# Second block of an attention kernel walked downwards, and its weight loads issued from ScalarE

## The chip, the cores and the metric

One core of a Trainium2 chip runs the whole program. The metric is the device time of one execution in microseconds; the kernel before was run three times, and the median counts.

## The reference, cut to what matters

The input is 16 sequences of 256 tokens with 256 features, in float32. One transformer layer is computed:

```
h   = layernorm(x)
q, k, v = h @ W_Q + b_Q, h @ W_K + b_K, h @ W_V + b_V     # 16 heads of 128
att = softmax(causal(q k^T / sqrt(128)))
y   = concat_heads(att v) @ W_O + b_O
x   = x + layernorm(y)
h   = layernorm(x)                                        # 256 -> 2048 -> 256
f   = (gelu(h @ Wg^T) * (h @ Wu^T)) @ Wd^T                # weights unpacked from 4-bit codes
x   = x + layernorm(f)
```

## The kernel before

**Precision.** Most products are made of float32 operands that are split into a high and a low part, so that one product is three matmuls (`mm3`: high*high, high*low, low*high). Splitting is an engine's work (a copy for the high part, a subtraction for the low part), so split weights are written to DRAM once and later loaded ready-made.

**Blocks, pairs, units.** The 4096 tokens are cut into `NBLK` = 8 blocks of `TB` = 512. Within a block the 16 heads are taken in `NG` = 8 pairs, and a pair gives two units, one for each head: 128 units in all. A numbered pair `p` is block `p // 8`, place `p % 8`; `head_pair(p)` says which two heads stand there. The main loop runs over `i`, one unit for each turn, as a software pipeline: in turn `i` the program records K and Q of unit `i+5` (`st_qk`), scores and softmax of unit `i+4` (`st_s`), V for unit `i+4` (`st_v`, or `st_v1` and `st_v2`), the transposition of the probabilities (`st_t`), the way of the transposed probabilities out to DRAM (`st_w`, four writes `hop<-tr`) and back (`st_b`, one load `pt<-hop`), their split (`st_p`), the product with V (`st_z`, whose result goes to `pz` and then through ScalarE to `zh`), and the product with W_O (`st_o`). After the attention come 32 groups of the feed-forward part, which use no K, Q or O weights and reuse V's and O's buffers.

**V.** V is computed for two head pairs at a time, over four units, under a key `w`. Keys of the first block (`w < 4`) use the plain form `st_v`: six matmuls of 512 columns in each of four units. Later keys use a form with seven products instead of eight (`st_v1`, `st_v2`): 42 matmuls of 256 columns over the four units, with sums in `vv` made by ScalarE and VectorE, and with the split left to `v_split` (ScalarE copies `vh`, GpSimd subtracts `vl`). Weights for the seven products are seven tiles wide (`WD[.., "v"]`, 896 KB for each part), for the plain form four.

**Weights.** Each of K and Q together (`WKQ`, 1024 KB), O (`WO`, 512 KB) and V (`WV`, two parts of 896 KB) has two buffers in SBUF. In block 0 the weights are made there and kept in DRAM (`w_keep`, `v_keep`, `v_keep_sums`). From block 1 on `w_get` loads them. The call `weights((p + 4, "kq"))` stands at the end of each even turn, `weights((p + 1, "o"), (p + 5, "v"))` at the end of each odd one. `DOWN` names the blocks that take the pairs in falling order: where a block falls and the one before it rises (or the reverse), the first two pairs and the first two V keys are those that still lie in the buffers, and `w_get` loads nothing for them (`back`). Before, `DOWN` is 2, 4, 6: block 1 rises like block 0 and begins with fresh loads.

**Order.** Every compute instruction goes through `run`, which holds it behind the instruction recorded last on each engine; every DMA goes through `dma`, which issues from SyncE (SP) and holds it behind the DMA issued last. So an engine's order, and SP's, is the order of the program. A DMA also takes one of eight semaphores in turn, and an issue waits until the DMA that last had the same semaphore has landed. Small jobs (layer norms, unpacking of feed-forward weights, sums) are fed in at `slot` calls.

Of the kernel before, what the change touches and what calls it, by code (L numbers as in the profile page):

```python
# [15 lines left out]
ALU = mybir.AluOpType  # L16
# [5 lines left out]
NBLK = NT // TB  # L22
NG = 8
# [5 lines left out]
def kernel(  # L29
# [19 lines left out]
    nc = tc.nc  # L49
# [11 lines left out]
    def f(ap):  # L61
        return ap.bitcast(F32)
# [24 lines left out]
    def dma(dst, src):  # L87
        if queue[0] is None:
            queue[0] = nc.sync.dma_start(dst, src).ins
            return  # L90
        with tc.issue_after(queue[0]):
            queue[0] = nc.sync.dma_start(dst, src).ins
# [3 lines left out]
    def run(op, dst, *args, **kw):  # L96
        with ExitStack() as behind:
            for m in last.values():
                behind.enter_context(tc.issue_after(m))
            ins = op(dst, *args, **kw)  # L100
        last[ins.ins.engine] = ins.ins
        return ins
# [23 lines left out]
    def add(jobs, job, kind):  # L126
        jobs.append([job, 0, kind])

    def overdue(time):
        while late and late[0][0] <= time:  # L130
            _, do, args = late.popleft()
            do(*args)
# [165 lines left out]
    W = {}  # L298
    RAW = {}
    WD = {}  # L300
# [2 lines left out]
    WO = wp.tile([P, 2, 2, 512], F32R, tag="wo", name="wo", bufs=1)  # L303
    WV = wp.tile([P, 2, 3584], F32R, tag="wv", name="wv", bufs=1)

    DOWN = range(2, NBLK, 2)

    def slot_of(p):
        return (p % NG + max(p // NG - 1, 0)) % 2

    def v_slot(w):
        return (w % (NG // 2) + max(w // (NG // 2) - 1, 0)) % 2

    def head_pair(p):
        b, at = divmod(p, NG)
        return NG - 1 - at if b in DOWN else at

    RAWV = {}

# [13 lines left out]
    def w_view(w):  # L333
        return w.rearrange("p s (k c) -> p s k c", k=2)
# [74 lines left out]
    def split(p, n):  # L409
        w_split(p, n)  # L410
        yield from ()

    def w_get(p, n):

        if p < NG:
            add(splits, split(p, n), A_ if n in "vo" else V_)
        elif p < len(pairs):
            overdue(now[0] + 4)
            g, back = head_pair(p), p % NG < 2 and p >= 2 * NG
            if n == "v":  # L420
                key, part = p // 2, p % 2
                at = key % (NG // 2)
                if at < 2 and p >= 2 * NG:
                    W[key, n] = W[key - 1 - 2 * at, n]
                    return
                W[key, n] = w = WV[:, v_slot(key)].rearrange("p (s m c) -> p s m c", s=2, m=7)
                dma(f(w[:, part]), WD[g // 2, n][:, part])
                return
            before = p - 1 - 2 * (p % NG)
            if n == "kq":  # L430
                w = WKQ[:, slot_of(p)]
                if not back:
                    dma(f(w), WD[g, n])
                for m in range(2):
                    W[p, n[m]] = W[before, n[m]] if back else w_view(w[:, m])
            else:
                w = WO[:, slot_of(p)]
                if not back:
                    dma(f(w), WD[g, n])
                W[p, n] = W[before, n] if back else w_view(w)  # L440

    MOVING_LAST = ((0, 0), (1, 0), (0, 1))
    STATIONARY_LAST = ((0, 0), (0, 1), (1, 0))
# [1 line left out]
    def mm3(o, terms, passes=STATIONARY_LAST, start=True, stop=True, shared=False, lows_last=False):  # L445

        todo = [(lhs(a), rhs(c)) for lhs, rhs in terms for a, c in passes]
        if lows_last:
            todo = [todo[m] for m in (0, 1, 3, 4, 2, 5)]
        for i, (lhs, rhs) in enumerate(todo):  # L450
            run(
                nc.tensor.matmul, o, lhs, rhs, start=start and i == 0, stop=stop and i == len(todo) - 1, skip_group_check=shared
            )


    units = [(b, NG - 1 - g if b in DOWN else g, j) for b in range(NBLK) for g in range(NG) for j in range(2)]
    N = len(units)
    pairs = [(b, g) for b in range(NBLK) for g in range(NG)]
    Q, K, V, PR, TR, HOP, PT, PH, Z, PO = {}, {}, {}, {}, {}, {}, {}, {}, {}, {}

    after = deque()
# [71 lines left out]
    def v_split(w, g, bi):  # L533
        c = slice(g * 256, (g + 1) * 256)
        vh, vl = (t[:, bi, c] for t in V[w][0:2])
        run(nc.scalar.copy, vh, vv[:, v_first(g, bi)])
        run(nc.gpsimd.tensor_tensor, vl, vv[:, v_first(g, bi)], f(vh), ALU.subtract)
# [26 lines left out]
    def st_v3(k):  # L564

        w, r = divmod(k, 4)
        w, g, bi = ((w - 1, 1, 0), (w, 0, 0), (w, 1, 1), (w, 0, 1))[r]
        if NG // 2 <= w < N // 4:
            v_split(w, g, bi)

    def st_v(k):
# [87 lines left out]
    def st_z(u):  # L659
        b, g, j = units[u]  # L660
        ph, pl, pt = PH.pop(u)
        vh, vl, vr = V[u // 4]
        at = 2 * (g % 2) + j
        e = slice(at * E, (at + 1) * E)
        pz = ps.tile([P, TB], F32, tag="pz", name="pz")
        for bi in range(2):
            o = pz[:, bi * S : (bi + 1) * S]
            mm3(o, [(lambda a: (vh, vl)[a][:, bi, e], lambda c: (ph, pl)[c][:, :, bi, :])], MOVING_LAST, stop=False)
            run(nc.tensor.matmul, o[:, P:], vr[:, bi, e], pt[:, 4 + bi], start=False, stop=True)
        zh = work.tile([P, TB], F32R, tag="zh", name="zh", bufs=3)  # L670
        zl = work.tile([P, TB], F32R, tag="zl", name="zl", bufs=3)
        bias = bqk[:, 2, 2 * g + j : 2 * g + j + 1]
        run(nc.scalar.activation, zh, pz, AF.Identity, bias=bias)
        after.append((nc.vector.scalar_tensor_tensor, zl, pz, bias, f(zh), ALU.add, ALU.subtract))
        Z[u] = (zh, zl)

    def st_o(p, dh):
# [151 lines left out]
    def f_tile(n):  # L829
        w = wp.tile([P, 2, 8, P], F32R, tag="fs", name="wu", bufs=2)  # L830
        if n == "d":
            return w.rearrange("p s m c -> p (s m c)")[:, 0:1024].rearrange("p (s k c) -> p s k c", s=2, k=2)
        return w

    FGD = {}

    def f_place(k, n):

        if n == "u":
            return f_tile(n)  # L840
        at = k + (n == "d")
        if at not in FGD:
            FGD[at] = WV[:, at % 2]
        if n == "g":
            return FGD[at][:, 0:2048].rearrange("p (s m c) -> p s m c", s=2, m=8)
        return FGD[at][:, 2048:3072].rearrange("p (s k c) -> p s k c", s=2, k=2)
# [351 lines left out]
    for i in range(-5, N + 2):  # L1198
        p = i // 2
        odd = i % 2 == 1  # L1200
        if p >= 0 and not odd and p < len(pairs):
            b, g = pairs[p]
            if g == 0 and b + 1 < NBLK:
                add(urgent, ln1(b + 1), N_)
            if b == 0 and g == 6:
                pieces = [(fg, n) for fg in range(NG) for n in "gud"]
                f_load(*pieces[0])
            if b == 0 and g == 7:
                for m, piece in enumerate(pieces):
                    add(idle, f_make(*piece, pieces[m + 1] if m + 1 < len(pieces) else None), V_)  # L1210
            if b == NBLK - 1 and g == 0:
                add(spare, x_ops(0), N_)
        if 0 <= i + 4 < N:
            st_s(i + 4)
        while after:
            run(*after.popleft())
        if 2 * NG <= i + 4 < N:
            st_v1(i + 4)
        slot(V_)
        if i + 5 < N:  # L1220
            st_qk(i + 5)
        else:
            finished.append(i)
        st_v3(i + 4)
        slot(V_, urgent, behind)
        slot(G_)
        slot(G_ + A_)
        if 0 <= i + 4 < N:
            st_t(i + 4)
        if i == N:  # L1230
            await_(X[0], "last", spare)
            X[0].pop("last")()
        if i >= N - 4:
            part(0, ("m1", "m2", "m6", "m5", "m7", "m3")[i - (N - 4)])
        if 0 <= p - 1 < len(pairs):
            st_o(p - 1, i % 2)
        if 0 <= i + 1 < N:
            st_p(i + 1)
        if 0 <= i + 4 < 2 * NG:
            st_v(i + 4)  # L1240
        elif 0 <= i + 4 < N:
            st_v2(i + 4)
        if 0 <= i < N:
            st_z(i)
        if 0 <= i + 3 < N:
            st_b(i + 3)
        if 0 <= i + 4 < N:
            st_w(i + 4)
        if odd:
            weights((p + 1, "o"), (p + 5, "v"))  # L1250
        else:
            weights((p + 4, "kq"))
        slot(A_ + G_)
        if N - 9 <= i < N - 7:
            f_get(0, "ug"[i - (N - 9)])
# [7 lines left out]
    for k in range(NGRP):  # L1263
        sb, g = divmod(k, NG)
# [88 lines left out]
```

## Time and profile before

| what | value |
|---|---|
| median of three runs | 1516.76 us (1514.41 to 1520.52) |
| the profiled execution, its own time | 1516.03 us |
| its span, first to last instruction | 1514.2 us |
| TensorE matmul (PE) busy | 1489.1 us, 98% |
| VectorE (DVE) / ScalarE (ACT) / GpSimd (POOL) busy | 1158.3 / 1111.2 / 728.3 us |
| moved by DMA | 391.89 MB, 76.7% of the time of 16 DMA engines on queue q1 |
| mean granted TensorE clock | 0.997 |
| loads and stores of `wkq` / `wo` | 52 / 52 issues from SP |
| seven-product loads of `wv` | 32 issues from SP |

Busy time of PE counts pipelined matmuls, so 98% says that PE seldom waits, not that it works at its peak. The profile is read here by the distance in time between equal points of two units: where nothing waits, that distance repeats exactly, and what a stretch has above it was lost. "SPq" is SP issuing a DMA.

### The profile page before, as it was taken

The numbers are of one execution on the slowest core, as the hardware profiler recorded it, in microseconds if no ns is written. First come the engines' busy times: TensorE is split into PE (matmuls) and PEld (weight loads), VectorE is DVE, ScalarE is ACT, GpSimd is POOL, SyncE is SP. The second block draws the span as 40 slices with busy tenths as digits, with TensorE's granted clock in tenths as the row PEclk, the third lists the DMA queues.
The fourth block names the chain that finished last, engine by engine and source line by source line (L and its number), as shares of the span: only waits on it lengthen the run. The fifth ranks groups of instructions, "written<-read, shape, count | busy, mean of one in ns | idle before, by whom it ended". The sixth has DMA issues, their size and how long they took to land.

```text
span 1514.2 us, 26690 instructions
## 1 busy us (share of the span) xinstructions
PE 1489.1 (98%) x8335; PEld 1297.3 (86%) x8335; DVE 1158.3 (76%) x3020; ACT 1111.2 (73%) x2804; POOL 728.3 (48%) x1041
## 2 busy tenths in 40 slices
PE   8999999999999999999999999999999999999997
PEld 7888888998899998899999889987888888888886
DVE  6775787777787787778778777767887787787876
ACT  6987777887887787787888777775666665666665
POOL 5876667767768867866786876630000000000000
PEclk9999999999999999999999999999999999999999
DMA  7999997898799699699789879875647465655561
GB/s 261 350 329 306 323 332 246 271 294 288 230 306 322 215 308 311 220 304 301 248 266 315 283 229 302 285 265 208 236 167 275 172 248 197 247 182 203 218 235 52
DMA packets 186991, 391.89 MB, mean 259 GB/s; under 512 B 19808, under 2 KB 127840, under 8 KB 169952
## 3 DMA queue, kind: packets, MB, share of 16 engines
q1 hardware_dynamic: 186848, 390.17, 76.7%
q8 instruction: 66, 1.08, 0.3%
q14 instruction: 77, 0.63, 0.1%
HBM read 275.28 MB, written 114.82 MB: 258 GB/s over the span
## 4 chain that ended last, share of the span: by engine, by line
PE 78%; DMA 9%; DVE 4%; POOL 3%; ACT 3%; issue 1%; SPq 1%; DVEq 0%; ACTq 0%; POOLq 0%
PE pd L100 13%; PE pk L100 9%; PE po L100 9%; PE pq L100 9%; PE pa L100 8%; PE pv L100 8%; PE pz L100 8%; PE sc L100 7%; PE pf L100 5%; PE pe L100 2%; DMA wv<-wv 2%; DVE sum L100 1%; DMA ohop<-oback 1%; POOL pr L100 1%; DMA o<-ohop 1%
## 5 line engine op out<-in xcount | busy, mean ns | idle before, releaser
L100 POOL TENSOR_SCALAR pr<-pr,rc 128x128 f32<-128x128 f32 (+1 forms) x512 | 219.6, 446 | 128.0 <-DVE rc L100 123.9
L100 DVE CUSTOM_DVE_ANT_0 sc<-sc,mask 128x128 f32<-128x128 f32 (+1 forms) x512 | 180.7, 374 | 114.9 <-PE sc L100 106.2
L100 POOL TENSOR_TENSOR rs<-rs,mhalf 128x4 f32<-128x4 f32 (+1 forms) x35 | 33.8, 965 | 480.6 <-DVE rs L100 271.8
L100 ACT ACTIVATE pr<-sc,mn 128x128 f32<-128x128 f32 (+1 forms) x512 | 207.8, 418 | 68.9 <-DVE mn L100 68.8
L100 PE MATMUL pv<-wv,xT 128*128 128x256 f32 (+1 forms) x1272 | 196.7, 291 | 3.1 <-DVE vv L100 2.9
L100 PE MATMUL pk<-xT,wkq 128*128 128x512 f32 x768 | 199.0, 394 | 0.4 <-DMA wkq<-wkq 0.4
L100 PE MATMUL pq<-xT,wkq 128*128 128x512 f32 x768 | 196.0, 391 | 0.0
L100 PEld LDWEIGHTS pv<-wv,xT 128*128 128x128 f32 x1272 | 177.8, 190 | 14.5 <-DVE vv L100 4.0
L100 PEld LDWEIGHTS pq<-xT,wkq 128*128 128x128 f32 x768 | 145.1, 189 | 30.9
L100 POOL TENSOR_TENSOR pl<-pt,ph 128x512 fp32r<-128x512 f32 x124 | 159.7, 1288 | 21.9 <-ACT ph L100 21.8
L100 ACT COPY part<-pa 128x512 f32<-128x512 f32 x192 | 111.6, 585 | 67.7 <-PE pa L100 65.0
L100 ACT ACTIVATE zh<-pz,bqk 128x512 fp32r<-128x512 f32 x128 | 88.4, 690 | 95.3 <-PE pz L100 95.0
L100 PE MATMUL po<-zh,wo 128*128 128x512 f32 x512 | 157.7, 389 | 0.0
L100 PEld LDWEIGHTS pk<-xT,wkq 128*128 128x128 f32 x768 | 136.3, 190 | 23.1 <-DMA wkq<-wkq 0.6
L100 DVE SCALAR_TENSOR_TENSOR kl<-pk,bqk,kh 128x512 fp32r<-128x512 f32 x128 | 95.7, 748 | 57.6 <-ACT kr L100 56.1
L100 POOL TENSOR_TENSOR vl<-vv,vh 128x256 fp32r<-128x256 f32 x112 | 83.4, 744 | 107.1 <-ACT vh L100 106.1
L100 DVE STREAM_TRANSPOSE tr<-pr 128x768 f32<-128x768 f32 x128 | 123.5, 965 | 6.6 <-DMA hop<-tr 5.4
L100 PEld LDWEIGHTS po<-zh,wo 128*128 128x128 f32 x512 | 96.1, 188 | 20.0
L100 PE MATMUL sc<-kr,qr 128*128 128x128 f32 x512 | 99.5, 275 | 6.1 <-ACT qr L100 6.1
L100 ACT ACTIVATION_READ_ACCUMULATOR pr<-sc,mn 128x1 f32 x512 | 103.9, 203 | 0.0
L100 DVE TENSOR_TENSOR sum<-sum 128x512 f32<-128x512 f32 x128 | 87.9, 686 | 17.9 <-ACT sum L100 17.6
L100 PE MATMUL po<-zl,wo 128*128 128x512 f32 x256 | 99.9, 390 | 0.9 <-DVE zl L100 0.9
(158 smaller groups left out, 3990.0 us busy)
## 6 DMA issues: line engine op xcount, KB each, us to landing
wkq<-wkq SPq DMA_DIRECT2D x52, 1024.0 KB, 6.4
hop<-tr SPq DMA_DIRECT2D x512, 96.0 KB, 3.7
pt<-hop SPq DMA_DIRECT2D x128, 384.0 KB, 5.2
wu<-fu SPq DMA_DIRECT2D x32, 1024.0 KB, 8.6
wv<-fg SPq DMA_DIRECT2D x32, 1024.0 KB, 5.7
wv<-wv SPq DMA_DIRECT2D x32, 896.0 KB, 6.5
wo<-wo SPq DMA_DIRECT2D x52, 512.0 KB, 4.7
wv<-fd SPq DMA_DIRECT2D x32, 512.0 KB, 3.5
```

Source lines behind the costliest of these rows:

```text
L100: ins = op(dst, *args, **kw)
```

## The change

1. `DOWN` becomes 1, 3, 5, 7. The order within a falling block keeps the two pairs of one V key in rising order (6, 7, 4, 5, 2, 3, 0, 1). Each block from 1 on now begins with the two pairs and the two V keys that lie in the buffers, so `back` holds for block 1 too; slots become `p % 2`.
2. The V keys 4 and 5 (the first half of block 1) are those of block 0 that still lie there in the plain form, so the plain form is used for six keys (`PLAIN = 6`) instead of four.
3. `w_get` issues its loads from ScalarE (`run(nc.scalar.dma_start, ...)`), in ScalarE's own order, instead of from SP. Loads drop from 44 + 44 + 32 (K/Q, O, V parts) to 42 + 42 + 28.
4. In the last five units the low part `zl` is recorded at once instead of at the start of the next turn.
5. The feed-forward buffers in `WV` swap places.

```diff
-    DOWN = range(2, NBLK, 2)
+    DOWN = range(1, NBLK, 2)
+    PLAIN = 6
     def slot_of(p):
-        return (p % NG + max(p // NG - 1, 0)) % 2
+        return p % 2
     def v_slot(w):
-        return (w % (NG // 2) + max(w // (NG // 2) - 1, 0)) % 2
+        return (w % (NG // 2) + w // (NG // 2)) % 2
     def head_pair(p):
-        return NG - 1 - at if b in DOWN else at
+        return NG - 2 - at // 2 * 2 + at % 2 if b in DOWN else at
...
     def w_get(p, n):
-            g, back = head_pair(p), p % NG < 2 and p >= 2 * NG
+            g, back = head_pair(p), p % NG < 2
...
-                if at < 2 and p >= 2 * NG:
+                if at < 2:
...
-                dma(f(w[:, part]), WD[g // 2, n][:, part])
+                run(nc.scalar.dma_start, f(w[:, part]), WD[g // 2, n][:, part])
...
-                    dma(f(w), WD[g, n])
+                    run(nc.scalar.dma_start, f(w), WD[g, n])
...
     def st_v3(k):
-        if NG // 2 <= w < N // 4:
+        if PLAIN <= w < N // 4:
...
     def st_z(u):
-        after.append((nc.vector.scalar_tensor_tensor, zl, pz, bias, f(zh), ALU.add, ALU.subtract))
+        low = nc.vector.scalar_tensor_tensor, zl, pz, bias, f(zh), ALU.add, ALU.subtract
+        if u + 5 < N:
+            after.append(low)
+        else:
+            run(*low)
...
-            FGD[at] = WV[:, at % 2]
+            FGD[at] = WV[:, (at + 1) % 2]
...
-        if 2 * NG <= i + 4 < N:
+        if 4 * PLAIN <= i + 4 < N:
             st_v1(i + 4)
...
-        if 0 <= i + 4 < 2 * NG:
+        if 0 <= i + 4 < 4 * PLAIN:
             st_v(i + 4)
```

More of the change, by code (lines that the diff above doesn't have):

```diff
@@ L426, in w_get @@
                 W[key, n] = w = WV[:, v_slot(key)].rearrange("p (s m c) -> p s m c", s=2, m=7)
-                dma(f(w[:, part]), WD[g // 2, n][:, part])
+                run(nc.scalar.dma_start, f(w[:, part]), WD[g // 2, n][:, part])
                 return
-            before = p - 1 - 2 * (p % NG)
             if n == "kq":
@@ L432, in w_get @@
                 if not back:
-                    dma(f(w), WD[g, n])
+                    run(nc.scalar.dma_start, f(w), WD[g, n])
                 for m in range(2):
-                    W[p, n[m]] = W[before, n[m]] if back else w_view(w[:, m])
+                    W[p, n[m]] = W[p - 2, n[m]] if back else w_view(w[:, m])
             else:
@@ L438, in w_get @@
                 if not back:
-                    dma(f(w), WD[g, n])
-                W[p, n] = W[before, n] if back else w_view(w)
+                    run(nc.scalar.dma_start, f(w), WD[g, n])
+                W[p, n] = W[p - 2, n] if back else w_view(w)
     MOVING_LAST = ((0, 0), (1, 0), (0, 1))
@@ L453, in mm3 @@
             )
-    units = [(b, NG - 1 - g if b in DOWN else g, j) for b in range(NBLK) for g in range(NG) for j in range(2)]
+    pairs = [(b, g) for b in range(NBLK) for g in range(NG)]
+    units = [(b, head_pair(p), j) for p, (b, _) in enumerate(pairs) for j in range(2)]
     N = len(units)
-    pairs = [(b, g) for b in range(NBLK) for g in range(NG)]
     Q, K, V, PR, TR, HOP, PT, PH, Z, PO = {}, {}, {}, {}, {}, {}, {}, {}, {}, {}
```

## The prediction

> **What bounds the kernel now.** I read the page first, for who is busy.
>
> ```profile
> span 1514.2 us, 26690 instructions
> ...
> PE 1489.1 (98%) x8335; PEld 1297.3 (86%) x8335; DVE 1158.3 (76%) x3020; ACT 1111.2 (73%) x2804; POOL 728.3 (48%) x1041
> ...
> DMA  7999997898799699699789879875647465655561
> ```
>
> PE is the bound: 98% busy, so only what makes PE wait, or gives it other matmuls, moves the end. The DMA row is near full in the first third of the span and falls later. Then I looked for where PE loses time. In the timeline I took the first weight load of each `pk` (one for each unit). Where nothing waits, four units of the seven-product form last 442.53 to 473.27 = 30.74 us, three of them 7.87. The view of windows, cut at such points (columns: length, then busy time of PE, PEld, DVE, ACT, POOL, then granted clock, DMA share, GB/s):
>
> ```profile
> 71.13:102.20 31.07, 31.07 (x179) 27.34 (x178) 22.98 (x66) 27.49 (x75) 22.91 (x30) 1.00 0.97 322
> 102.20:135.48 33.28, 32.41 (x185) 28.23 (x183) 19.91 (x63) 23.73 (x67) 22.16 (x31) 1.00 0.97 319
> 135.48:228.93 93.45, 92.77 (x584) 83.53 (x583) 69.36 (x210) 72.19 (x204) 64.39 (x93) 1.00 0.97 324
> 228.93:248.43 19.50, 17.64 (x103) 15.49 (x102) 12.21 (x41) 13.18 (x37) 14.66 (x21) 0.91 0.93 317
> 248.43:356.33 107.90, 107.77 (x679) 97.28 (x678) 85.35 (x259) 85.87 (x243) 73.97 (x109) 1.00 0.84 266
> 356.33:851.13 494.80, 493.55 (x3107) 446.03 (x3105) 389.35 (x1183) 395.22 (x1107) 362.40 (x524) 1.00 0.87 280
> ```
>
> Row 1 is four plain units with PE never idle: 31.07. Row 2 is four more plain units: 2.2 us lost. Row 3 is twelve units, 3 x 30.74 = 92.22: 1.2 lost. Row 4 is two units, 2 x 7.87 = 15.74: 3.8 lost, at a granted clock of 0.91. So the stretch that ends with the first units of block 2 loses 7.2 us, with DMA at 0.93 to 0.97. After it, row 5 loses 0.6 against 14 units (123.0 - 15.7 = 107.3), row 6 loses 2.8 against 16 x 30.74 = 492.0, and 851.13 to 976.26 loses 2.1: 5.5 us in six blocks.
>
> Next I asked what ends the waits. At the entrance of block 1 the timeline of SP and ACT shows fresh loads in the way:
>
> ```profile
> 109.74 0.45 SPq L92 DMA_DIRECT2D wv<-wv  x1
> ...
> 120.49 0.34 SPq L92 DMA_DIRECT2D wkq<-wkq  x1
> ...
> 121.15 0.63 ACT L100 ACTIVATE wo<-rawo 128x512 fp32r<-128x512 f32 x1 [3.58 <-DMA rawo<-in_wo]
> ```
>
> The chain goes through just these two: the `wv` load took 10.73 us, SP waited for it before `wkq` (120.49), and PE's `pk` waited for that at 126.96. Behind the same `wv`, `rawo` was late, and ACT sat 3.58 us in front of its softmax. At the end of block 1 the chain reads:
>
> ```profile
> 222.61 7.97 DMA o<-ohop
> ...
> 230.60 5.84 DMA hop<-tr
> ...
> 236.62 0.98 DVE tr L100
> ...
> 238.22 0.98 PE pv L100 x6
> ```
>
> A `hop` write waits its turn, the transpose waits for its buffer, DVE's `vv` is late and PE stands still for 1.86 us (timeline). From 239.76 on, for 3.4 us, the granted clock is 0.5, which makes up most of the rest of row 4's 3.8.
>
> **The change part by part.** *Block 1 falls.* Removed: two `wkq`, two `wo` and four `wv` loads, 2 x 1024 + 2 x 512 + 4 x 896 = 6656 KB = 6.8 MB, the last of them issued at 187.40 us. At row 2's 319 GB/s that is 21 us of transfer out of the 126 us from 102.20 to 228.93. Row 2's loss hangs on two of these loads: gone, -2.2. For row 3 the waits are of DVE's `vv` at 186 and 190 us, where SP is 5 to 7 us behind its place in the program: `wkq` is issued at 179.80, its turn's `zh` ended at 173.2. With less queued, -1.2. Row 4's loss has the `o` load, two `xs` loads and an `fu` store in front of the `hop` write, and none of these is removed; but SP came there late (`wo` issued at 220.41, its turn's `zh` ended at 213.0), and in later blocks the same place costs far less: row 6 holds four such places and loses 2.8 in all. I take the whole 3.8 as gone, because a wait that ends before 1.86 us takes the clock's part with it; the bounds are 0 and 3.8.
>
> The granted clock fell after a PE gap of 1.86 us. The page "TensorE: Matmul & The Clock Gate" of the Trainium skill (Part 1: The HAM clock gate) gives an idle window of about 3.4 us as what drops the clock to half. By that rule this gap would have cost only its 1.9 us, and the sum below would be 1.9 us smaller in gain; the trace, with 0.91 in row 4, decides.
>
> *Two keys become plain.* Row 1 against the steady four units: 31.07 - 30.74 = 0.33 for each key, on the path since PE has no gap there: +0.7 for two. What this takes from the others (for a key four `vl` at 0.74 us from POOL, about 1 us net from ACT and 1.3 us net from DVE) is beside PE and counted at nothing; it only adds slack.
>
> *Loads leave SP.* 112 issues. SP's take 0.34 to 0.45 us, median 0.44: 49 us that SP no longer spends in 900. SP mostly waits, for example for `hop` landings (171.6 us in its waits), so its issue time is not the bound in the steady blocks. At the six block ends SP holds the loads back behind a wait for `oback` and `ohop` (up to 10 us after the turn's `zh`); the loads are freed from that, but PE waited for a load there only once (0.13 us at 355.75). The other way round, `hop` and `pt` are freed from the loads in front of them. I take 1 of the 5.5 us of the later blocks as gained; the bounds are 0 and 3, since 2.1 us of PE's waits are for POOL's `vl`, which is not SP's.
>
> The page "DMA: Bandwidth & Descriptors" (section "Issuing engines are not separate DMA queues") speaks against this part: transfers issued by two engines share the 16 DMA engines, and only issue time is saved. By that rule this part is 0 and the gain 1 us smaller.
>
> *ACT issues.* No DMA is issued by ACT in the trace, so the price is bounded: nothing, or SP's 0.44 us each, 49 us of ACT. The place is after `zh`, ahead of the next unit's four `pr` exponentials, `kh`, `kr`, `qh`, `qr` and `ph`, which all queue behind it. There ACT is idle in most turns:
>
> ```profile
> 664.85 0.69 ACT L100 ACTIVATE zh<-pz,bqk 128x512 fp32r<-128x512 f32 x1 [0.81 <-PE pz L100]
> 666.41 0.37 ACT L100 ACTIVATE pr<-sc,mn 128x128 f32<-128x128 f32 x1 [0.87 <-DVE mn L100]
> ```
>
> One issue (even turns) or two (odd) take 0.44 or 0.88 of that 0.87. Behind it `qr` ends at 163.05 and PE wants it at 164.47 (timeline of block 1): 1.4 us more. So up to 0.87 + 1.4 = 2.3 us in a turn cost nothing; I take 0, being nearest to the 0.88. No wait on PE comes with it: the buffers' last readers run ahead of `pz` in PE's order, which `zh` has waited for. What comes is the wait for the eighth DMA before it. In the changed program's order that is in most cases a `hop` write of the turn before, landed long before (median 3.7 us), and never one that stands behind the `ohop` of the same turn.
>
> The loads now start up to 2 us earlier, beside the `hop` writes (660.10 against a `zh` end of 658.4). At 323 GB/s a `wkq` is 3.2 us; a `hop` delayed by that still lands within the two turns (15.7 us) that two `tr` buffers give. Cost 0; it becomes real where DVE's `tr` waits, four times and 5.4 us in all before.
>
> *`zl` at once, `WV` swapped.* VectorE's order in the two built programs is the same at the end, since nothing was recorded between the two places: the 0.9 us wait of PE for `zl` at 1006 stays. 0 for both.
>
> Sum: -2.2 - 1.2 - 3.8 + 0.7 - 1.0 = -7.5. The profiled execution took 1516.03 (span 1514.2 and 1.8 around it), 0.7 under the median of the runs. 1516.03 - 7.5 = **1508.5 us**.
>
> **The rivals.** *Half of it stays.* Row 4 is made by `o`, `xs` and `fu` ahead of `hop`, which the change leaves in SP's queue, and the second queue brings nothing. Then -2.2 - 1.2 + 0.7 = -2.7, or -1.5 if row 3 stays as well: 1513 to 1514.5, no change that counts. For it: the chain names those three, no weight load. Against: the steady blocks have the same three and lose little.
>
> *More comes back.* The loads' own queue also empties SP at every block end: 3 of the 5.5 us there, and the sum is -9.5: 1506.5 or somewhat less.
>
> *ACT becomes the waiter (slower).* One mechanism: an issue on ACT waits for a landing that SP itself has delayed, and everything behind `zh` waits with it. SP is 7 to 10 us late at each of six block ends (`wo` at 349.5, its turn's `zh` ended at 340.1). If ACT inherits half of that, 4 us, less the 2.3 us of cover, it costs 1.7 us in each of three turns at each of six ends, 31 us; less the gain of 7.5: 1539.5, and with two of the three turns 1529. It decides from 2.3 us of wait in a turn on. For it: ACT is 73% busy and keeps strict order; a PE gap of 2 us also costs clock. Against: the program's order of the eighth DMA before, as above.
>
> **How the numbers follow.** The forecast has 0.46; its own range is 1505.5 to 1511.5. Half stays: 0.20. More comes back: 0.15. ACT waits: 0.19. About 0.5% is what a measurement of this kernel can tell from no change, 7.6 us from the median, which is 1509.2 and 1524.3. The forecast lies across the first: 0.30 of its 0.46 faster, 0.16 the same. Half stays is all the same, more comes back all faster, ACT waits 0.17 slower and 0.02 the same. So faster has 0.30 + 0.15 = 0.45, the same 0.16 + 0.20 + 0.02 = 0.38, slower 0.17. The range 1503 to 1521 takes in the first three cases with the bounds of their terms and leaves out most of the last.
>
> **What would show it.** Right: windows of block 1 at 31.07 for plain units and 30.74 for the others; DMA share in block 1 near 0.81 (0.97 x 34.2 MB / 41.0 MB) instead of 0.97; no wait of ACT for `rawo`; no granted clock under 1 at 240 us; PE's wait for `vv` gone from its list. Wrong: new waits of PE for ACT `qr` or POOL `vl`, idle time in front of ACT's `pr` ended by a DMA, DVE's `tr` waiting for `hop` more than four times, or units above 7.87 us in blocks 2 to 7 where they were even.

## The result, and the profile after

The changed kernel takes 1593.53 us (median of 4 runs, 1586.86 to 1596.16) where the kernel before takes 1516.63 in the same comparison: ratio 1.0499, 95% interval 1.0465 to 1.0532 (times are medians, ratios go by means). The forecast was 1508.5, range 1503 to 1521. The profiled execution took 1592.19 us. Its page:

```profile
span 1590.4 us, 26600 instructions
...
PE 1516.5 (95%) x8299; PEld 1312.9 (83%) x8299; DVE 1156.1 (73%) x3016; ACT 1111.2 (70%) x2798; POOL 723.2 (45%) x1033
...
DMA  8996886887789588778868868886664664664652
...
q1 hardware_dynamic: 169568, 291.60, 54.6%
q10 hardware_dynamic: 16128, 91.76, 17.5%
```

PE has 36 matmuls fewer than before and is busy 27.4 us longer (1516.5 against 1489.1); it is idle for 73.9 us (1590.4 - 1516.5) against 25.1. So of 76.2 us of span, 48.8 are PE standing still and 27.4 are longer matmuls: 0.7 by the forecast's price for the two plain keys, the rest at a lower clock. The other engines work as long as before, ACT to the tenth (1111.2): no engine has more to do. The DMA row is lower, not fuller. `q10` is the new queue of the loads.

Where it is lost, in windows cut at the first weight load of a unit's `pk`, as in the forecast (length, busy time of PE, PEld, DVE, ACT, POOL, then granted clock, DMA share, GB/s):

```profile
102.34:133.42 31.08, 31.08 (x179) 27.34 (x178) 19.13 (x60) 23.85 (x67) 22.19 (x31) 1.00 0.76 259
133.42:232.73 99.31, 96.06 (x555) 84.33 (x554) 65.98 (x204) 69.66 (x196) 58.68 (x85) 0.98 0.81 264
232.73:257.64 24.91, 19.31 (x102) 16.44 (x101) 13.79 (x46) 14.36 (x39) 14.72 (x21) 0.86 0.75 240
257.64:372.05 114.41, 109.73 (x679) 98.34 (x678) 82.98 (x251) 85.36 (x240) 73.59 (x108) 0.99 0.81 257
372.05:915.62 543.57, 511.76 (x3107) 457.88 (x3105) 389.12 (x1185) 396.31 (x1108) 363.01 (x524) 0.97 0.79 253
```

A block is counted here as in the forecast's rows, which begin three units ahead of its own first K: "block 2's first two units" are those with `pk` of units 29 and 30, counted from 0, while the output of block 0 comes back through DRAM (`ohop`, `o`).

The entrance of block 1 is even, as forecast. But block 2's first two units take 24.91 where they took 19.50, and blocks 3 to 6 take 543.57 where they took 494.80. In the timeline most units still take 7.87 or 7.15 us; the loss sits at each block's first two units (up to 14.81) and around its units 10 to 13 (up to 16.75). The view of waits says, for the whole span (total us, times, longest):

```profile
PE pv L100 <- DVE vv L100: 39.1, 20, 5.3
PE po L100 <- DVE zl L100: 12.8, 6, 5.7
...
DVE tr L100 <- DMA hop<-tr: 61.2, 29, 5.0
...
SPq L92 <- DMA hop<-tr: 255.3, 166, 7.4
SPq L92 <- DMA wkq<-wkq: 110.9, 25, 9.1
SPq L92 <- DMA wo<-wo: 79.3, 27, 5.4
SPq L92 <- DMA wv<-wv: 41.9, 13, 6.6
```

PE waits for DVE's `vv` and `zl`, DVE stands in front of `tr` until an older `hop` write has landed (29 times, four before), and SP waits 65 times, 232 us, for weight loads that it no longer issues. The chain shows why that matters, at the second half of block 3:

```profile
442.49 0.02 ACT zh L100
...
442.55 8.22 DMA wkq<-wkq
...
450.78 0.40 SPq L92
...
452.71 0.42 SPq L92
...
453.95 4.32 DMA hop<-tr
...
458.66 0.88 DVE tr L100
...
462.17 0.70 DVE vv L100
...
462.92 1.65 PE pv L100 x6
```

and SP's own timeline of the same time:

```profile
443.42 0.39 SPq L92 DMA_DIRECT2D fu<-wu  x1
450.78 1.29 SPq L92 DMA_DIRECT2D xs<-in_x  x2
452.31 0.34 SPq L92 DMA_DIRECT2D pt<-hop  x1
452.71 3.04 SPq L92 DMA_DIRECT2D hop<-tr  x4
```

SP issues nothing from 443.81 to 450.78. The `xs` load that it then issues has no data in common with `wkq`; it goes 0.02 us after the `wkq` load, issued by ACT, has landed. Behind it stand `pt` and the four `hop` writes. The built program says what ties them: completions of all DMAs that SP and ACT issue are counted on eight semaphores in turn, so a DMA may only go when the one eight places before it, in whichever queue, has landed. 96 of SP's DMAs carry such a wait for a load of ACT's, 48 of them `hop` writes and 18 `pt` loads.

### The profile page after: what moved, and what is told of

Read it like the earlier page. It is cut to its first block, busy times and chain, and to the rows that moved or that the text cites. A ratio compares the mean times of both kernels' runs of the same rounds, so it can differ in the third digit from the quotient of the medians.

```text
span 1590.4 us, 26600 instructions
## 1 busy us (share of the span) xinstructions
PE 1516.5 (95%) x8299; PEld 1312.9 (83%) x8299; DVE 1156.1 (73%) x3016; ACT 1111.2 (70%) x2798; POOL 723.2 (45%) x1033
## 4 chain that ended last, share of the span: by engine, by line
PE 65%; DMA 21%; DVE 5%; ACT 3%; SPq 2%; issue 2%; POOL 1%; DVEq 0%; ACTq 0%; POOLq 0%
PE pd L100 12%; DMA hop<-tr 9%; PE pa L100 8%; PE pk L100 7%; PE pq L100 7%; PE pv L100 7%; PE po L100 7%; PE pz L100 6%; PE pf L100 5%; PE sc L100 5%; DMA wkq<-wkq 3%; SPq L92 2%; PE pe L100 2%; DMA wo<-wo 2%; DMA xs<-in_x 2%; DMA pt<-hop 2%
## 5 line engine op out<-in xcount | busy, mean ns | idle before, releaser
L100 PE MATMUL pv<-wv,xT 128*128 128x256 f32 (+1 forms) x1236 | 203.0, 301 | 42.7 <-DVE vv L100 39.1
L100 PE MATMUL pk<-xT,wkq 128*128 128x512 f32 x768 | 208.1, 408 | 0.1
L100 PE MATMUL pq<-xT,wkq 128*128 128x512 f32 x768 | 201.4, 399 | 0.0
L100 PEld LDWEIGHTS pq<-xT,wkq 128*128 128x128 f32 x768 | 150.2, 196 | 33.1
L100 PEld LDWEIGHTS pk<-xT,wkq 128*128 128x128 f32 x768 | 142.4, 198 | 24.1 <-ACT xT L100 0.3
L100 POOL TENSOR_TENSOR vl<-vv,vh 128x256 fp32r<-128x256 f32 x104 | 77.6, 746 | 114.8 <-ACT vh L100 107.5
```

## The experiments

Two theories for the loss stood against each other, A (the shared turn of completions) and B (the two queues share the transfer engines), and C, that the queue is not the cause.

**1. The loads back in SP's queue, all else as changed.**

```diff
-                    run(nc.scalar.dma_start, f(w), WD[g, n])
+                    dma(f(w), WD[g, n])
```

(The same for V's part.)

> The changed kernel with the weight loads back in SyncE's queue; the downward second block, the six plain V keys and the zl edit stay. Theories for the loss of 77 us: A, completion turns: the program counts the completions of all its DMAs on eight counters in turn, so a DMA may only be issued when the one eight places before it, in whichever queue, has landed; a load that ScalarE issues late and that takes 7 us to land holds SyncE in the middle of the hop writes. B, shared transfer engines: the loads' packets in a second queue slow the packets of hop and pt. C, the downward second block itself (other keys, other slots) makes the loss. A and B expect the forecast's block-1 gains and no loss: 1508.5 us, 1503 to 1514. C expects about 1590 us.

Measured: 1506.24 us (5 runs), ratio 0.9932, 0.9915 to 0.9949. C falls. The two parts of the change have opposite signs: all that is not the queue brings some 10 us, the queue, without that gain, costs 87 (1593.5 - 1506.2). This is the fastest of the kernels here that compute the whole. Its windows, block 2's first two units and blocks 3 to 6:

```profile
226.65:244.19 17.54, 16.01 (x103) 14.35 (x102) 12.19 (x41) 12.99 (x37) 14.60 (x21) 1.00 0.89 299
...
351.44:843.38 491.94, 491.94 (x3106) 445.54 (x3105) 391.06 (x1185) 396.05 (x1108) 363.16 (x524) 1.00 0.88 281
```

In blocks 3 to 6 PE never stands.

**2. The queue alone, on the kernel before.** The same three calls, the other way round, in the kernel before.

> The kernel before with nothing changed but the issuer of the weight loads from the second block on: ScalarE in place of SyncE. A and B expect the whole loss without the block-1 gains: 1590 to 1605 us, SyncE waiting some 200 us or more for wkq, wo and wv loads. C expects 1517 us, as before.

Measured: 1607.81 us, ratio 1.0606 (1.0583 to 1.0630). That is the whole loss without the gain of experiment 1, and 3 us above the range of A and B; SP waits 189 us for loads, where some 200 were expected.

**3. The loads issued earlier.** `weights(...)` is called ahead of `st_z` instead of at the turn's end, from pair 4 on.

> The changed kernel with each load issued by ScalarE ahead of the turn's zh instead of behind it, that is some 2 to 4 us earlier in a turn of 7.87 us. Bytes, queue and packets are the same. A: SyncE waited 232 us for such loads in some 65 waits of 3.6 us; with a load issued 2 to 4 us sooner most of these waits go, and the time falls to between 1515 and 1550 us. B: the same transfers share the engines as before, 1580 to 1600 us.

Measured: 1563.07 us, ratio 1.0293 (1.0269 to 1.0318); SP's waits for loads 138 us in place of 232. 30 of the 87 us come back for a move of a few us with the same bytes in the same queue. That is 13 us above A's range and 17 below B's; alone it does not decide.

**4. The loads issued by GpSimd.**

```diff
-                    run(nc.scalar.dma_start, f(w), WD[g, n])
+                    run(nc.gpsimd.dma_start, f(w), WD[g, n])
```

> The changed kernel with the loads issued by GpSimd in a third kind of queue, whose completions the program counts apart from SyncE's and ScalarE's: no SyncE DMA waits for a load that it has nothing to do with. The bytes and the separate queue stay. A: the loss goes, 1503 to 1520 us (what GpSimd pays for an issue is not known; it is busy about half of the time). B: the packets still share the engines, 1580 to 1600 us.

Measured: 1533.51 us (6 runs, 1525.67 to 1537.31), ratio 1.0096 (1.0071 to 1.0122): neither range. In this program the completions of GpSimd's loads are counted apart; SP's waits for loads are gone from its list, and some 60 of the 87 us with them. 27 us stay. The profiled execution took 1525.74, so its trace holds some 20 of them. What it shows is `hop` at work beside the loads (issue to landing at the end of the row; 3.6 us in experiment 1) and what DVE's `tr` waited for it:

```profile
hop<-tr SPq DMA_DIRECT2D x512, 96.0 KB, 4.8
```

```profile
  DMA hop<-tr: 16.7, 8
```

The eight waits lie at block starts, where `ohop`, `o`, `xs` and the loads meet: block 4's first unit takes 11.47 us after `hop` writes of 10.55 and 6.68 us in the chain.

**5 and 6. A quarter of the bytes.** Of each load only the first quarter, `f(w[:, 0, 0])`, `f(w[:, 0, 0:256])`, for V `f(w[:, part, 0:2])`; issued by ACT in the one, by GpSimd in the other. (GpSimd also clears, once, the part of V's buffers that is then never loaded.)

> The changed kernel, ScalarE issuing the loads, but each load brings only the first quarter of its bytes (two sevenths for V; the rest of the weights is what the place held before, so that the output is not the reference's). With the loads in SyncE's queue the time was 1506 us, with ScalarE as the issuer 1593 us. A (completion turns): a load still holds SyncE until it has been issued behind zh and has landed, but it lands in about 3 us in place of 7, so a part stays: 1515 to 1555 us, SyncE still waiting for the loads some 50 to 150 us. B (shared transfer engines): a quarter of the bytes, at most a quarter of the 87 us: 1506 to 1528 us, and SyncE's waits for the loads gone.

> The same quarter loads issued by GpSimd. With whole loads this issuer gave 1533 us, 27 above the loads in SyncE's queue. B as the cause of these 27 us (hop writes that land in 4.8 us in place of 3.6 beside the loads): 1504 to 1515 us. What GpSimd pays to issue, or its place in GpSimd's order, as the cause: 1525 to 1537 us, as with whole loads.

Measured: ACT 1529.42 us, ratio 1.0091 (1.0076 to 1.0106); GpSimd 1505.78 us, ratio 0.9935 (0.9918 to 0.9951). With GpSimd as the issuer the 27 us are gone: they were bytes, not the issuing (B). It ends level with experiment 1, which suggests that in SP's queue the loads cost nothing that is left to gain; no run has quarter loads there. With ACT as the issuer some 23 us stay, at the same bytes: that is the tie to SP (A). The split depends on what is taken away first. Experiments 4 and 6 gave 60 us for the tie and 27 for the bytes; here, with the tie kept, a quarter of the bytes gives back 64 us (1593.5 - 1529.4), and the tie has the other 23. The two work through each other: a load with fewer bytes lands sooner, and so lets SP go sooner. But one expectation of A was wrong, the sum of SP's waits:

```profile
SPq L92 <- DMA wo<-wo: 92.9, 26, 7.8
SPq L92 <- DMA wv<-wv: 92.2, 21, 8.6
SPq L92 <- DMA wkq<-wkq: 83.2, 23, 6.9
```

268 us, more than the 232 of the change, for a quarter of its loss. So the length of a wait in a queue is no price. A reading that fits, not shown by itself: SP arrives earlier and waits longer until ACT gets to its `zh`; what costs is how long after that the load lands (`wkq` 4.3 us here, 7.0 in the change), since the `hop` write behind it is needed by a fixed time.

**7. The tie without bytes.** Experiment 1, and at each of the 112 loads ACT issues a DMA of 64 bytes to a tile in DRAM that nobody reads.

```diff
+        ticks.append(dram.tile([1, 16], F32, name=f"tick{len(ticks)}"))
+        run(nc.scalar.dma_start, ticks[-1], bqs[0:1])
```

> The loads in SyncE's queue (1506 us), and in addition, at each of the 112 loads, ScalarE issues a DMA of 64 bytes at the place where the change issues the load. It carries no bytes to speak of, moves none of the loads and only takes a turn among the eight completion counters. A: SyncE waits for ScalarE's late little DMAs, which land in perhaps 2 to 3.6 us after zh: 1515 to 1555 us. B: no bytes, no loss, 1505 to 1509 us.

Measured: 1568.62 us, ratio 1.0348 (1.0332 to 1.0365). 112 DMAs with 7 KB in all cost 62 us (1568.6 - 1506.2); B can't explain that. SP's list:

```profile
SPq L92 <- PE pd L100: 286.0, 27, 15.5
SPq L92 <- DMA tick<-bqs: 212.6, 68, 6.2
```

It is more than A's range, and a part of it runs on another path than in the change: here SP still issues the loads, and PE waited 31.9 us (8 times) for `wv` loads that a held SP issued late. So the run shows that the tie alone is enough to cost tens of us, not that it makes 62 of the 87.

**8. The order inside a key.** The kernel before, with one more part of the change: downward blocks take the head pairs as 6, 7, 4, 5, ... in place of 7, 6, 5, 4, ...

```diff
-        return NG - 1 - at if b in DOWN else at
+        return NG - 2 - at // 2 * 2 + at % 2 if b in DOWN else at
```

(With the slots and the kept weights that follow from it.)

> The kernel before (second block upwards, loads in SyncE's queue) with one more part of the change that the forecast gave no price: in a downward block the two head pairs of a V key keep their order (6, 7, 4, 5, ...) where the kernel before turns them round (7, 6, 5, 4, ...). The changed kernel with SyncE's loads gained 3.9 us in blocks 3 to 7 where the forecast had 1.0 for a reason that was not even there (SyncE free of loads). If this order is where they come from: 1511 to 1514 us, blocks 3 to 7 at 122.99 us each and no wait of PE for vl after a falling block. If they come from the downward second block: 1516 to 1518 us, as before.

Measured: 1510.26 us (12 runs, 1507.94 to 1517.48), ratio 0.9971 (0.9958 to 0.9984): 0.7 us below the range for this order. In its profiled execution (1508.93 us) blocks 3 to 7 take 122.99 us each, without a lost unit, and PE's wait for `vl` (2.1 us before) is gone. The slower of the twelve runs are not explained by it.

## Why the prediction was wrong

**The step that failed** is *ACT issues*: "What comes is the wait for the eighth DMA before it." It looked at the tie from one side, how long a load of ACT's waits for SP's DMA eight places before, and found that harmless. The other side was not asked: which of SP's DMAs stands eight places behind a load, and when that load lands. ACT issues it only behind its turn's `zh`, and it lands about a turn later (`wkq` 7.0 us, turn 7.87; the forecast had reckoned 3.2 from the rate, where the page of before has 6.4 from issue to landing). SP's `hop` writes of the next turns stand behind that. While the loads were in SP's queue the same turn was harmless, because a load was issued when SP came to it. The built program and the landing times of before held all of this.

From there the other steps follow:

- *Loads leave SP*, -1.0: the sign was wrong. The change against experiment 1 is +87 us; about 60 go when the tie goes (4), 27 when the bytes go as well (6); in the other order 64 and 23 (5). So no fixed share belongs to either. Experiment 4 also changes the issuer and the kind of queue (the profile lists GpSimd's as `q0 software_dynamic`, ACT's as `q10 hardware_dynamic`), and no run has whole loads in ACT's queue without the tie. The page "DMA: Bandwidth & Descriptors" of the Trainium skill (section "Issuing engines are not separate DMA queues") says that issuing from several engines saves only issue time. The runs agree that nothing is gained, but it is not a zero: GpSimd's queue cost 27 us with whole loads and nothing with a quarter of the bytes.
- *The hop delayed beside loads*, cost 0: the condition given, DVE's `tr` waiting more than four times, came true: 29 times in the change, 8 in experiment 4. The two `tr` buffers did not cover a `hop` that is issued late and lands late.
- *ACT's issue time*, 0 within 0 to 49 us: nothing speaks against it. An issue took 0.33 us from 442.55 on, while `zh` ran from 442.49 to 443.18, and ACT's busy time is the same.
- *The rival "ACT becomes the waiter"* had the sign, not the mechanism, and asked for a rise of 13 to 23 us. It is SP that waits, though the delay comes round to ACT: ACT's `ph` waits 27.9 us for `pt` (2.8 before), and behind it in the chain, at 232.85, ACT issues the `wo` load that holds SP next.

*The steps on block 1*, read from experiment 1, where nothing covers them. The entrance (-2.2) came, but it was read too large: 0.71 of it was the step from plain to seven-product keys (a unit of 8.48 in place of 7.77), which moves to unit 11 and stays. Block 1 as a whole went from 126.74 to 124.66 us, -2.1, against -2.7 (-2.2 - 1.2 + 0.7).

Experiment 8 shows how loose these terms are: up to row 4 its instructions are those of the kernel before, yet rows 2 to 4 took 31.78, 94.66 and 18.34 us in its profiled execution where they had taken 33.28, 93.45 and 19.50. Of the 7.2 us that the forecast read as lost there, 5.8 were lost this time, and at the entrance nothing but the step of 0.71. So what of these gains is the change's work is known to some 1.5 us only.

*Row 4*, -3.8: it gave 2.0 (19.50 to 17.54). PE still stands 1.53 us for `vv` there, as the first rival said of this row; only the clock's part went. *Later blocks*, counted as above: -4.5 in blocks 2 to 7 (107.90 to 107.25, and 619.93 to 616.05), where -1.0 had been given to the freed SP. Experiment 8 has the same even blocks 3 to 7 from the order inside a key alone, which the forecast did not price at all. So without the queue the kernel is at 1506.2, near the 1508.5, but as a sum of terms that were too large and one that was missing: that it comes so near is luck.

*Signs.* The DMA share in block 1 is 0.76 and then 0.81 (0.81 expected; luck, since the block was stretched: in experiment 1 it is 0.80 and then 0.89) and ACT's wait for `rawo` is gone; PE's wait for `vv` grew from 2.9 to 39.1 us, and the clock, which was to stay at 1.00, was 0.86 in the stretch of row 4. Of the signs for "wrong", the `hop` waits and the uneven units came; PE's wait for `qr` stayed (5.6 us), and none for `vl` is left.

## What to carry to other kernels

When some of a queue's DMAs get another issuer, look for what still ties the two queues, and in both directions: list for each DMA that stays what it waits for in the built program, when that is issued now, and when it lands. Here a long load in the same queue, behind the small urgent writes, let these land in 3.6 us (experiment 1); in a queue of its own it was at work beside them, and they took 4.8 (experiment 4). And run the parts of a mixed change apart: here a gain of 0.7% was buried under a loss of 5.7%.

## What the runs showed of the hardware

The granted clock fell after short waits, as after the one of 1.86 us that the forecast had read. In the change PE stood still for over 1.2 us twelve times between 225 and 1060 us: after the one of 1.62 us the mean clock of the next 7 us stayed at 1.00, after five between 1.79 and 2.64 us it was 0.75 each time, after the six of 4.09 us and more 0.53 to 0.76. It is no fixed limit: in experiment 2 it was 0.75 after 1.77 us and 1.00 after 2.42 us, in experiment 4 1.00 after 3.46 us. The page "TensorE: Matmul & The Clock Gate" of the Trainium skill (Part 1: The HAM clock gate) gives an idle window of about 3.4 us for a drop; here drops also came after waits of 1.77 to 2.64 us, so these rows do not show that limit. Over the span the clock is 0.981 in place of 0.997, about 25 us of 1590 (an estimate: 0.016 x 1590), which is nearly all of the 27.4 us that PE's matmuls took longer: about a third of the 76 us is the clock's answer to the waits.
